# Layer 0's feed-forward with its modulation and gate moved to ScalarE, between transposes

## The chip, the core and the metric

The kernel runs on one core of a Trainium2 chip. The metric is device time in microseconds for one execution of the whole program. The engines are named by their units: TensorE (PE in the profile, PEld for its weight loads), VectorE (DVE), ScalarE (ACT), GpSimd (POOL) and SyncE (SP, here only for transfers).

## The reference, cut to what matters

Two transformer layers with adaptive layer norm, on x of 8 batches x 512 tokens x 128 features, in float32. Each layer adds a gated attention and then a gated feed-forward. The change is in layer 0's feed-forward, whose linear layers quantise inputs and weights to four-bit floats in blocks of 16 features:

```python
def fp4_quant_dequant(x):
    xb = x.reshape(shape[:-1] + (shape[-1] // 16, 16))
    scale = jnp.max(jnp.abs(xb), axis=-1, keepdims=True) / 6.0
    scale = jnp.maximum(scale, jnp.float32(1e-12))
    xn = xb / scale
    idx = jnp.searchsorted(_MID, jnp.abs(xn))
    q = _GRID[idx] * jnp.sign(xn) * scale      # grid 0, 0.5, 1, 1.5, 2, 3, 4, 6
    return q.reshape(shape)

def fp4_linear(x, w):
    return jnp.einsum('bsk,nk->bsn', fp4_quant_dequant(x), fp4_quant_dequant(w))

# layer 0, feed-forward: 128 -> 352 -> 128
h = _layernorm(x, axis=-1) * (1 + cb) + sb     # sb, cb, gb: 128 values per batch
gate, y = fp4_linear(h, w_gate), fp4_linear(h, w_up)
x = x + gb * fp4_linear(jax.nn.silu(gate) * y, w_down)
```

The six vectors per batch (sa, ca, ga for attention, sb, cb, gb for the feed-forward) come from one small product with a conditioning input.

## The kernel before

The residual stream X lies in SBUF for the whole run, tokens in rows (partitions): for each of the 8 batches, NT = 4 tiles of 128 tokens x 128 features. The run has four stages one after the other: layer 0's attention (to 156 us), layer 0's feed-forward (158 to 307 us), layer 1's attention (to some 920 us), and layer 1's feed-forward.

In layer 0's attention a scheduler orders the instructions of each engine by data and by its own costs. In layer 0's feed-forward the order is the one written out in the program (`tc.manual_schedule()`), so an engine that waits for one instruction holds all that stand behind it in its queue.

The modulation vectors exist in two forms. `modT[0]` has features in partitions, one column per kind and batch. `modb[0]` has them laid out as rows, the same in every partition: `mod_rows` makes them per batch, with a diagonal tile on GpSimd (L353), a matmul with ones (L358) and a copy by ScalarE (L362), for four kinds: attention's gate, the feed-forward's shift, scale and gate.

The feed-forward of a batch goes through these parts, each of class `Ffn0`:

- `norm`: ScalarE normalises the four tiles into `n` (L295); GpSimd multiplies by the scale row (L589) and adds the shift row (L590).
- `Fp4.scales` on VectorE: maxima per block of 16 (L426), scale (L430), its reciprocal (L433, L436). The input of one batch and the hidden `y` of an earlier one share these instructions.
- `Fp4.scaled`: the input times its reciprocal scales, on GpSimd (L439). `octaves`: an Abs on ScalarE (L446). `rounded`: two passes on VectorE (L450, L451). `back`: times the scales (L454), on VectorE for the input, on GpSimd for `y` in most batches.
- `turn`: four transposes (L311) into PSUM and a copy by ScalarE (L596) to `hT`, features in partitions.
- `products(t)` for each of four token tiles: gate and up matmuls (L609, L610), SiLU on ScalarE (L612), their product on VectorE (L613) into `y`, 352 features per token.
- `y` is quantised as the input was.
- `down(t)`: four transposes of 88 x 128 (L627) and a copy by ScalarE (L628) to `yT`.
- `gated`: GpSimd multiplies the down weights by the batch's gate row (L634). `last(t)`: the down projection (L640) into PSUM tile `pd`, tokens in rows. `end`: VectorE adds it to X (L647).

The batches are pipelined. In step i the loop works on batch i-1 (`past`: down projection), i (`cur`: rounding of `y`), i+1 (`new`: products), i+2 (`far`: quantising and turning the input) and i+3 (`next_far`: norm). The inputs of the first AHEAD = 3 batches are already quantised during layer 0's attention, where they are called `hq`; the others are called `n_f`. Between these parts, some steps place work of layer 1's first batch (`more_front`): norms, projections and products of line coordinates, the latter on GpSimd (L756). After each batch's `end`, VectorE takes layer 1's statistics of it (L231, L232), in front of the next step's `scales`. After the loop, a hand-written tail treats batches 6 and 7.

PSUM has four buffers of tag "mm" (products), two of "tp" (transposes) and two of "acc" (`pd`).

Of the kernel before, what the change touches and what calls it, by code (L numbers as in the profile page):

```python
# [11 lines left out]
F32 = mybir.dt.float32  # L12
# [3 lines left out]
AF = mybir.ActivationFunctionType  # L16
ALU = mybir.AluOpType
AX = mybir.AxisListType
PSUM = bass.MemoryType.PSUM

P = 128
# [17 lines left out]
def kernel(ctx: ExitStack, tc: tile.TileContext, a: dict, out: bass.AP):  # L39
# [15 lines left out]
    def acc(name):  # L55
        return four.tile([P, 512], F32, tag="acc", bufs=accs, name=name)
# [160 lines left out]
    class Stats:  # L217


        def __init__(self, tag):  # L220
            self.tag, self.mv, self.rstd, self.nb = tag, [], [], []
# [85 lines left out]
    def transposed(src, name, pt=None):  # L307

        pt = tp(name) if pt is None else pt
        for t in range(NT):  # L310
            nc.tensor.transpose(pt[:, t * P : (t + 1) * P], src[:, t, :], ident)  # L311
        return pt
# [34 lines left out]
    def mod_rows(l, b):  # L347

        mb = modb[l][:, b]
        nch = mb.shape[1]  # L350
        cols = modT[l][:, 2:6, b] if l == 0 else modT[l][:, 2::3, b]
        diag = sp.tile([P, nch, P], F32, tag=f"diag{l}", bufs=1, name=f"diag{l}_{b}")
        nc.gpsimd.tensor_mul(  # L353
            diag, ident.unsqueeze(1).to_broadcast([P, nch, P]),
            cols.unsqueeze(2).to_broadcast([P, nch, P]),
        )
        pb = mm(f"modb{l}_{b}")
        nc.tensor.matmul(  # L358
            pb[:, : nch * D], lhsT=ones, rhs=diag.rearrange("p j d -> p (j d)"),
            start=True, stop=True,  # L360
        )
        nc.scalar.copy(mb.rearrange("p j d -> p (j d)"), pb[:, : nch * D])  # L362

    modulation(0, wmod0, 4)
    nc.sync.dma_start(out=wmod1, in_=a["wmod1"])


# [14 lines left out]
    def rows(ap, n):  # L382

        return ap.unsqueeze(1).to_broadcast([ap.shape[0], n, D])
# [12 lines left out]
    class Fp4:  # L397

        def __init__(self, pool, src, np_, n, name):
            self.pool, self.np_, self.n, self.name, self.x = pool, np_, n, name, src
            self.blocks = src.rearrange("p (g k) -> p g k", k=16)

        def over(self, v):
            return v.unsqueeze(2).to_broadcast([self.np_, self.n // 16, 16])
# [6 lines left out]
        def scales(self, *more):  # L413

            all_ = (self, *more)
            num = [q.n // 16 for q in all_]
            nb, np_ = sum(num), self.np_
            amax, scale, rs = (
                self.pool.tile(
                    [P, nb], F32, tag=f"q_{tag}_b{nb}", bufs=bufs, name=f"q_{tag}_{self.name}"  # L420
                )[:np_]
                for tag, bufs in (("amax", 1), ("scale", 2), ("rs", 2))
            )
            parts = [slice(sum(num[:i]), sum(num[: i + 1])) for i in range(len(num))]
            for q, part in zip(all_, parts):
                nc.vector.tensor_reduce(  # L426
                    amax[:, part], q.blocks, AX.X, ALU.max, apply_absolute_value=True
                )
                q.scale, q.rs = scale[:, part], rs[:, part]
            nc.vector.scalar_tensor_tensor(  # L430
                scale, amax, 1.0 / 6.0, tiny[:np_].to_broadcast([np_, nb]), ALU.mult, ALU.max
            )
            nc.vector.reciprocal(rs, scale)  # L433


            nc.vector.scalar_tensor_tensor(rs, rs, 2.0 ** -24 - 1.0, rs, ALU.mult, ALU.min)  # L436

        def scaled(self, eng=nc.gpsimd):
            eng.tensor_mul(self.blocks, self.blocks, self.over(self.rs))  # L439

        def octaves(self):

# [136 lines left out]
    class Ffn0:  # L579
# [5 lines left out]
        def norm(self, n=None):  # L585

            b = self.b
            self.n = n = ln_norm(self.pool, "f0", self.stats, b, n)
            nc.gpsimd.tensor_mul(n, n, rows(modb[0][:, b, 2, :], NT))  # L589
            nc.gpsimd.tensor_add(n, n, rows(modb[0][:, b, 1, :], NT))  # L590
            self.qh = Fp4(self.pool, n.rearrange("p t d -> p (t d)"), P, NT * D, f"h_{b}")

        def turn(self):
            pt = transposed(self.qh.x.rearrange("p (t d) -> p t d", d=D), f"q0T_{self.b}")
# [34 lines left out]
                self.yT[:, :, t * P : (t + 1) * P], pt[:CH0].rearrange("p (c q) -> p c q", q=P)  # L629
            )  # L630

        def gated(self):
            self.wd = self.pool.tile([CH0, NC0, D], F32, tag="wd", name=f"wd_{self.b}")
            nc.gpsimd.tensor_mul(self.wd, w0[2], rows(modb[0][:CH0, self.b, 3, :], NC0))  # L634

        def last(self, t):
            if t == 0:
                self.po = acc(f"pd_{self.b}")
            for c in range(NC0):
                nc.tensor.matmul(  # L640
                    self.po[:, t * P : (t + 1) * P], lhsT=self.yT[:, c, t * P : (t + 1) * P],
                    rhs=self.wd[:, c, :], start=(c == 0), stop=(c == NC0 - 1),
                )

        def end(self):
            xb = X[:, self.b * NT : (self.b + 1) * NT, :]
            nc.vector.tensor_add(xb, xb, self.po.rearrange("p (t d) -> p t d", d=D))  # L647

    flag = const.tile([1, 1], I32, name="flag")
    nstats, w0, f0 = Stats("f0"), [], []  # L650
# [157 lines left out]
    with tc.tile_pool(name="p_f0", bufs=2) as pool, tc.manual_schedule():  # L808
        for f in f0:
            f.pool = pool  # L810
        f0 += [Ffn0(pool, b, stats) for b in range(AHEAD, B)]


        front, lines = fronts1(keep, st, 0, nstats, packs)
        steps = {
            2: ((front,), (front,)),
            3: ((front,), (front,)),
            4: ((lines,), (front,)),
            5: ((lines,), (front,)),
            6: ((lines,), (lines, lines, front)),  # L820
        }

        def f0_at(i):
            return f0[i] if 0 <= i < B else None

        for i in range(-2, B - 1):
            past, cur, new, far, next_far = (f0_at(i + k) for k in range(-1, 4))

            def more_front(half):
                for series in steps.get(i, ((), ()))[half]:
                    next(series)

            open_ = far if far and far.b >= AHEAD else None
            if next_far and next_far.b < AHEAD:
                next_far = None
            quants = (cur.qy if cur else []) + ([open_.qh] if open_ else [])
            if quants:
                quants[0].scales(*quants[1:])  # L840
            if open_:
                open_.qh.scaled()
            if cur:
                cur.qy[0].scaled()
                cur.gated()
            if new:
                new.products(0)
                new.products(1)
            if next_far:
                next_far.norm()  # L850
            if past:
                past.down(0)
                past.down(1)
            if open_:
                open_.qh.octaves()
                open_.qh.rounded()
                open_.qh.back(nc.vector)
            more_front(0)
            if new:
                new.products(2)  # L860
            if past:
                past.last(0)
                past.down(2)
            if new:
                new.products(3)
            if past:
                past.last(1)
                past.down(3)
            if i == B - 2:
                new.qy[0].scales()  # L870
                new.qy[0].scaled(nc.vector)
            if cur:
                cur.qy[0].octaves()
                cur.qy[0].rounded()
                cur.qy[0].back(nc.vector if i > B // 2 else nc.gpsimd)
            if past:
                past.last(2)
            if far:
                far.turn()
            if past:  # L880
                past.last(3)
                past.end()
            more_front(1)
            if past:
                nstats.after(past.b)


        past, cur = f0[B - 2 :]
        qa, qb = cur.qy
        cur.gated()  # L890
        act_tables()
        qa.octaves()
        past.down(0)
        past.down(1)
        qb.scales()
        qb.scaled()
        qa.rounded()
        qa.back(nc.vector)
        next(lines)
        past.last(0)  # L900
        past.down(2)
        past.last(1)
        past.down(3)
        qb.octaves()
        qk_packs(packs, 1)
        past.last(2)
        past.last(3)
        past.end()
        next(lines)
        next(lines)  # L910
        cur.down(0)
        cur.down(1)
        qb.rounded()
        qb.back(nc.vector)
        cur.last(0)
        cur.last(1)
        next(front)
        cur.down(2)
        nstats.after(past.b)
        cur.last(2)  # L920
        cur.down(3)
        cur.last(3)
        cur.end()
        nstats.after(cur.b)
    stats = nstats
# [740 lines left out]
```

## Time and profile before

| | |
|---|---|
| runs | 1119.83, 1113.53 and 1120.34 us; median 1119.83 |
| profiled execution | 1115.72 us, of which 1114.0 us are the span of the profile |
| busy, share of the span | PE 87%, DVE 73%, PEld 66%, ACT 51%, POOL 45% |
| mean granted TensorE clock | 0.954 |
| layer 0's feed-forward | 158 to 307 us |

The span reaches from the first to the last instruction. Busy shares are means over all four stages, which differ in what limits them. Lines of instructions give the start, the time, engine, source line, operation, output and inputs with their shapes, and in brackets how long the engine stood idle before and what released it. The granted clock is TensorE's; 0.50 is half of full speed.

### The profile page before, as it was taken

What the parts mean: (1) busy time and instruction counts of PE and PEld (TensorE: products, weight loads), DVE (VectorE), ACT (ScalarE), POOL (GpSimd) and SP (SyncE); (2) the same over time, 40 slices, a digit from 0 to 9 for tenths busy, and PEclk for the clock granted to TensorE, in tenths of its full rate; (3) what the DMA queues carried; (4) which work ended last, traced back from release to release, by engine and by line L of the source; (5) the groups of instructions that cost most, each with busy time, mean ns of one, the idle gap of its engine ahead of it and who ended that gap; (6) DMA issues with size and microseconds to landing.
All of it is one profiled execution on the core that took longest, in us unless ns stands there. A gap on an engine that the chain in (4) does not pass through costs nothing.

```text
span 1114.0 us, 24810 instructions
## 1 busy us (share of the span) xinstructions
PE 966.2 (87%) x10474; PEld 730.2 (66%) x10474; DVE 812.1 (73%) x1548; ACT 571.8 (51%) x863; POOL 502.1 (45%) x577
## 2 busy tenths in 40 slices
PE   5788886867678999999999989999988887999996
PEld 3566654655545677767777677677766675787885
DVE  7887968999847778787787877877877836645633
ACT  4736444644422545555545455454545447867743
POOL 4436217774456666576665665656644400000000
PEclk9899999898757999999999999999999999999998
DMA  6011000000000000000000000000000000000001
GB/s 174 29 39 29 1 1 1 1 1 1 1 0 1 2 3 2 2 2 3 2 2 2 3 2 2 2 2 2 2 2 2 2 2 1 1 1 20 19 1 40
DMA packets 14713, 11.19 MB, mean 10 GB/s; under 512 B 2246, under 2 KB 13062, under 8 KB 14598
## 3 DMA queue, kind: packets, MB, share of 16 engines
q1 hardware_dynamic: 13878, 8.96, 2.8%
q8 instruction: 84, 1.38, 0.5%
q10 hardware_dynamic: 720, 0.60, 0.2%
q14 instruction: 31, 0.25, 0.1%
HBM read 7.46 MB, written 2.10 MB: 9 GB/s over the span
## 4 chain that ended last, share of the span: by engine, by line
PE 52%; DVE 15%; ACT 14%; POOL 11%; issue 6%; DMA 1%; SPq 0%; POOLq 0%; ACTq 0%; DVEq 0%
PE ph L1134 11%; ACT pr L1071 7%; PE s L1056 6%; PE s L1016 6%; PE s L1044 5%; PE pi L989 3%; POOL kd L970 3%; PE po L1085 3%; POOL bias L1005 2%; PE py L494 2%; PE s L501 1%; POOL m L756 1%; DVE pack_q L1033 1%; PE po L1534 1%; PE pmT L944 1%
## 5 line engine op out<-in xcount | busy, mean ns | idle before, releaser
L1071 ACT ACTIVATE pr<-s 128x1024 f32<-128x1024 f32 (+1 forms) x192 | 169.0, 880 | 237.4 <-PE s L1056 237.4
L1033 DVE TENSOR_REDUCE pack_q<-s 128x2 f32<-128x256 f32 (+3 forms) x256 | 205.4, 824 | 6.6
L1056 PE MATMUL s<-qm,kd 32*128 32x128 f32 x2560 | 195.0, 286 | 0.0
L1016 PE MATMUL s<-kd,qd 31*128 31x256 f32 (+3 forms) x1024 | 187.3, 475 | 2.4 <-POOL bias L1005 1.5
L1030 DVE TENSOR_TENSOR s<-s,bias 128x256 f32<-128x256 f32 (+1 forms) x192 | 99.4, 517 | 84.9 <-PE s L1056 63.9
L1056 PEld LDWEIGHTS s<-qm,kd 32*128 32x128 f32 x2560 | 158.4, 187 | 1.3 <-issue 1.3
L1044 PE MATMUL s<-ident,bias 128*128 128x128 f32 x512 | 96.2, 290 | 46.3 <-ACT pr L1071 42.5
L1005 POOL TENSOR_SCALAR_AFFINE_SELECT bias<-bias 128x512 f32<-128x512 f32 x128 | 77.8, 634 | 102.0 <-DVE bias L1001 101.7
L970 POOL TENSOR_TENSOR kd<-k1T,dk 128x512 f32<-128x512 f32 (+3 forms) x128 | 106.7, 866 | 37.7 <-ACT k1T L961 37.7
L1044 PEld LDWEIGHTS s<-ident,bias 128*128 128x128 f32 x512 | 55.4, 141 | 92.3 <-ACT pr L1071 79.1
L1134 PE MATMUL ph<-g,h 128*128 128x512 f32 x448 | 106.7, 396 | 0.0
L1016 PEld LDWEIGHTS s<-kd,qd 31*128 31x128 f32 x1024 | 83.9, 189 | 33.5 <-issue 20.1
L1001 DVE TENSOR_TENSOR bias<-pi,wdiag 128x512 f32<-128x512 f32 x128 | 79.5, 683 | 34.6 <-PE pi L989 34.6
L1134 PEld LDWEIGHTS ph<-g,h 128*128 128x128 f32 x448 | 83.7, 188 | 19.9
L1085 PE MATMUL po<-pr,pack_v 128*32 128x128 f32 x2560 | 89.8, 276 | 3.9 <-DVE o L1105 3.7
L951 POOL TENSOR_TENSOR qd<-q1T,dq 128x512 f32<-128x512 f32 x32 | 40.6, 1269 | 88.4 <-ACT q1T L939 88.4
L1085 PEld LDWEIGHTS po<-pr,pack_v 128*32 128x32 f32 x2560 | 64.4, 109 | 17.6 <-PE s L1056 5.8
L989 PE MATMUL pi<-k1L,q1T 31*128 31x128 f32 x1024 | 54.7, 288 | 0.9 <-DVE pack_q L1033 0.9
L989 PEld LDWEIGHTS pi<-k1L,q1T 31*128 31x128 f32 x1024 | 47.8, 195 | 8.0 <-issue 7.2
L1524 DVE TENSOR_TENSOR g<-g2v,g 128x1024 fp32r<-128x1024 f32 x16 | 19.6, 1226 | 38.2 <-ACT g L1520 38.2
L951 POOL TENSOR_TENSOR qm<-m1T,dq 128x512 f32<-128x512 f32 x32 | 40.6, 1270 | 13.7 <-ACT m1T L978 13.7
L439 POOL TENSOR_TENSOR y<-y,q_rs_y 128x1408 f32<-128x1408 f32 (+1 forms) x8 | 20.1, 2510 | 46.0 <-DVE q_rs_y L436 23.5
(332 smaller groups left out, 1973.1 us busy)
## 6 DMA issues: line engine op xcount, KB each, us to landing
X<-in_x SPq DMA_DIRECT2D x8, 256.0 KB, 4.1
w<-in_h SPq DMA_DIRECT2D x8, 256.0 KB, 2.6
out_x<-X SPq DMA_DIRECT2D x8, 256.0 KB, 2.3
w<-in_w SPq DMA_DIRECT2D x3, 256.0 KB, 4.5
wmod<-in_wmod ACTq DMA_DIRECT2D x1, 384.0 KB
wmod<-in_wmod SPq DMA_DIRECT2D x1, 384.0 KB, 5.3
c_wqkv<-in_wqkv ACTq DMA_DIRECT2D x1, 192.0 KB, 5.6
c_wA<-in_wA SPq DMA_DIRECT2D x1, 192.0 KB, 4.5
```

The source lines that it names most:

```text
L951: nc.gpsimd.tensor_mul(qd, qT.rearrange("p (t q) -> p t q", q=P), dq[:, g, :].unsqueeze(1).to_broadcast([P, NT, P]),)
L970: nc.gpsimd.tensor_mul(kd[t], kT[:, : (t + 1) * P], dk[:, g, 384 - t * P :])
L989: nc.tensor.matmul(pi[:, j, tile_t], lhsT=qT[rl, tile_t], rhs=kL[rl, tile_t], start=True, stop=True,)
L1005: nc.gpsimd.affine_select(out=bias[:, j], in_=bias[:, j], compare_op=ALU.is_ge, fill=NEG, base=0, pattern=[[0, NT], [-1, P]], channel_mult ...
L1016: nc.tensor.matmul(s[:, j, at : at + (t + 1) * P], lhsT=st["qd", b, g][rk, t, :], rhs=st["kd", b, g][t][rk, :], start=True, stop=True,)
L1030: nc.vector.tensor_add(diag, diag, tiles)
L1033: nc.vector.tensor_reduce(packs["q", b % 2][:, t, h : h + 2, KM], s[:, :, at : at + (t + 1) * P], AX.X, ALU.max, negate=True,)
L1044: nc.tensor.matmul(p[:, j, at + t * P : at + (t + 1) * P], lhsT=bias[:, j, t, :], rhs=ident, is_transpose=True, start=(n == 0), stop=False ...
L1056: nc.tensor.matmul(p[:, j, at + k * P : at + (k + 1) * P], lhsT=st["kd", b, g][t][rk, k * P : (k + 1) * P], rhs=st["qm", b, g][rk, t, :], ...
L1071: nc.scalar.activation(pr[:, :, :end], st["p", b, g, u, i][:, :, :end], AF.Exp)
L1085: nc.tensor.matmul(po[32 * j : 32 * j + 32, t * P : (t + 1) * P], lhsT=vp[:, k, h * VW : h * VW + 32], rhs=st["pr", b, g, u, j // 2][:, j ...
L1134: nc.tensor.matmul(dst[:, j], lhsT=w, rhs=src[part][:, j], start=first and part == 1, stop=last and part == 0,)
```

## The change

Shift, scale and gate of layer 0's feed-forward are applied by ScalarE with features in partitions, where they are one scale and one bias per partition, instead of by GpSimd with rows.

- For batches 3 to 7, `norm` ends after ScalarE's normalising. A new part `modulated` transposes the normalised tiles (TensorE, four transposes), and ScalarE applies scale and shift while it moves them out of PSUM into a tile `m`. A new part `turned_back` transposes `m` back, into a PSUM tile of tag "acc". The quantiser takes its maxima from this PSUM tile and its scaling reads it and writes to SBUF; this scaling is now on VectorE (`scaled(nc.vector)`).
- The down projection swaps its operands, so that `pd` has features in partitions; it uses the plain down weights. `gated` is now a ScalarE activation that multiplies `pd` by the gate into a tile `o`; `end` transposes `o` (four transposes) and VectorE adds that PSUM tile to X.
- The gate is no longer laid out as a row: `mod_rows` makes three kinds for layer 0.
- The order in the loop: `y`'s scaling comes first on GpSimd; the third `products` and the first `more_front` come ahead of the input's rounding; `modulated` ahead of the rounding of `y`; the last two `last` and `gated` ahead of `turn`; `turned_back` behind it. In the tail, batch 6's `end` comes behind the first `down` of batch 7.

```diff
-        cols = modT[l][:, 2:6, b] if l == 0 else modT[l][:, 2::3, b]
+        cols = modT[l][:, 2:5, b] if l == 0 else modT[l][:, 2::3, b]
...
-    modulation(0, wmod0, 4)
+    modulation(0, wmod0, 3)
...
-        def __init__(self, pool, src, np_, n, name):
-            self.pool, self.np_, self.n, self.name, self.x = pool, np_, n, name, src
-            self.blocks = src.rearrange("p (g k) -> p g k", k=16)
+        def __init__(self, pool, src, np_, n, name, dst=None):
+
+            self.pool, self.np_, self.n, self.name = pool, np_, n, name
+            self.x = src if dst is None else dst
+            self.src, self.blocks = (
+                ap.rearrange("p (g k) -> p g k", k=16) for ap in (src, self.x)
+            )
...
-                    amax[:, part], q.blocks, AX.X, ALU.max, apply_absolute_value=True
+                    amax[:, part], q.src, AX.X, ALU.max, apply_absolute_value=True
...
         def scaled(self, eng=nc.gpsimd):
-            eng.tensor_mul(self.blocks, self.blocks, self.over(self.rs))
+            eng.tensor_mul(self.blocks, self.src, self.over(self.rs))
...
             self.n = n = ln_norm(self.pool, "f0", self.stats, b, n)
+            if b >= AHEAD:
+                return
             nc.gpsimd.tensor_mul(n, n, rows(modb[0][:, b, 2, :], NT))
...
+        def modulated(self):
+
+            pt = transposed(self.n, f"nT_{self.b}")
+            self.m = self.pool.tile([P, NT, P], F32, tag="m", bufs=1, name=f"m_{self.b}")
+            nc.scalar.activation(
+                self.m.rearrange("p t q -> p (t q)"), pt, AF.Identity,
+                bias=modT[0][:, 3, self.b : self.b + 1], scale=modT[0][:, 4, self.b : self.b + 1],
+            )
+
+        def turned_back(self):
+            name = f"mT_{self.b}"
+            pt = transposed(self.m, name, acc(name))
+            self.qh = Fp4(
+                self.pool, pt, P, NT * D, f"h_{self.b}", self.n.rearrange("p t d -> p (t d)")
+            )
...
-        def gated(self):
-            self.wd = self.pool.tile([CH0, NC0, D], F32, tag="wd", name=f"wd_{self.b}")
-            nc.gpsimd.tensor_mul(self.wd, w0[2], rows(modb[0][:CH0, self.b, 3, :], NC0))
-
...
-                    self.po[:, t * P : (t + 1) * P], lhsT=self.yT[:, c, t * P : (t + 1) * P],
-                    rhs=self.wd[:, c, :], start=(c == 0), stop=(c == NC0 - 1),
-                )
+                    self.po[:, t * P : (t + 1) * P], lhsT=w0[2][:, c, :],
+                    rhs=self.yT[:, c, t * P : (t + 1) * P], start=(c == 0), stop=(c == NC0 - 1),
+                )
+
+        def gated(self):
+            self.o = self.pool.tile([P, NT, P], F32, tag="o", bufs=1, name=f"of_{self.b}")
+            nc.scalar.activation(
+                self.o.rearrange("p t q -> p (t q)"), self.po, AF.Copy,
+                scale=modT[0][:, 5, self.b : self.b + 1],
+            )
 
         def end(self):
             xb = X[:, self.b * NT : (self.b + 1) * NT, :]
-            nc.vector.tensor_add(xb, xb, self.po.rearrange("p (t d) -> p t d", d=D))
+            pt = transposed(self.o, f"oT_{self.b}")
+            nc.vector.tensor_add(xb, xb, pt.rearrange("p (t d) -> p t d", d=D))
...
-            if open_:
-                open_.qh.scaled()
             if cur:
                 cur.qy[0].scaled()
-                cur.gated()
+            if open_:
+                open_.qh.scaled(nc.vector)
...
+            more_front(0)
+            if new:
+                new.products(2)
             if open_:
                 open_.qh.octaves()
                 open_.qh.rounded()
                 open_.qh.back(nc.vector)
-            more_front(0)
-            if new:
-                new.products(2)
...
+            if next_far:
+                next_far.modulated()
...
             if past:
                 past.last(2)
+                past.last(3)
+                past.gated()
             if far:
                 far.turn()
+            if next_far:
+                next_far.turned_back()
             if past:
-                past.last(3)
                 past.end()
...
         past.last(3)
-        past.end()
+        past.gated()
         next(lines)
         next(lines)
         cur.down(0)
+        past.end()
         cur.down(1)
...
         cur.last(3)
+        cur.gated()
         cur.end()
```

More of the change, by code (lines that the diff above doesn't have):

```diff
@@ L889 @@
         qa, qb = cur.qy
-        cur.gated()
         act_tables()
```

## The prediction

> **What bounds the kernel now.** I read the page first (busy shares, the 40 slices), then the chain of work that ended last, then stretches of some 18 us with their busy times, then the timeline of one stretch engine by engine, and the answers by source line. The page says that TensorE leads over the whole run, which hides that the stage the change touches, layer 0's feed-forward, has another limit:
>
> ```profile
> span 1114.0 us, 24810 instructions
> ...
> PEclk9899999898757999999999999999999999999998
> ```
>
> The feed-forward runs from 158 to 307 us. Its busy times by stretch (columns: length, then busy us and count of PE, PEld, DVE, ACT, POOL, then the granted clock) show VectorE full and TensorE not:
>
> ```profile
> 194.00:212.00 18.00, 14.68 (x69) 11.61 (x70) 16.39 (x23) 11.73 (x23) 13.61 (x10) 0.73 0.00 0
> 212.00:230.00 18.00, 14.97 (x89) 11.59 (x87) 16.61 (x25) 10.53 (x21) 12.71 (x7) 0.98 0.00 1
> 250.00:272.00 22.00, 15.22 (x80) 11.93 (x81) 20.47 (x30) 10.69 (x21) 8.98 (x7) 0.84 0.00 0
> ```
>
> The chain agrees: in this stage it runs almost wholly through VectorE. Here is VectorE in the step whose reciprocal scales are ready at 216.36 us, and GpSimd beside it:
>
> ```profile
> 216.08 0.28 DVE L436 SCALAR_TENSOR_TENSOR q_rs_y<-q_rs_y 128x120 f32<-128x120 f32 x1
> 216.28 0.94 DVE L613 TENSOR_TENSOR y<-silu,pu 128x352 f32<-128x352 f32 x2
> 218.20 2.40 DVE L450 SCALAR_TENSOR_TENSOR n_f<-q_big_h,n_f 128x512 f32<-128x512 bf16 x1 [0.97 <-ACT q_big_h L446]
> 220.64 1.64 DVE L451 SCALAR_TENSOR_TENSOR n_f<-q_big_h,n_f 128x512 f32<-128x512 bf16 x1
> 222.31 1.65 DVE L454 TENSOR_TENSOR n_f<-n_f,q_scale_y 128x512 f32<-128x512 f32 x1
> 223.88 0.94 DVE L613 TENSOR_TENSOR y<-silu,pu 128x352 f32<-128x352 f32 x2
> 224.75 1.83 DVE L450 SCALAR_TENSOR_TENSOR y<-q_big_y,y 128x1408 f32<-128x1408 bf16 x1
> 226.61 1.62 DVE L451 SCALAR_TENSOR_TENSOR y<-q_big_y,y 128x1408 f32<-128x1408 bf16 x1
> ```
>
> ```profile
> 217.46 2.59 POOL L439 TENSOR_TENSOR y<-y,q_rs_y 128x1408 f32<-128x1408 f32 x1
> 220.01 1.71 POOL L634 TENSOR_TENSOR wd<-wdT,mb 88x512 f32<-88x512 f32 x1
> 221.69 1.72 POOL L589 TENSOR_TENSOR n_f<-n_f,mb 128x512 f32<-128x512 f32 x1
> 223.49 1.60 POOL L590 TENSOR_TENSOR n_f<-n_f,mb 128x512 f32<-128x512 f32 x1
> ```
>
> Three passes over 512 columns take 2.40, 1.64 and 1.65 us; they end at 220.60, 222.28 and 223.96, each 0.55 after one of GpSimd's ends (220.05, 221.72, 223.41). The same L450 elsewhere, and L613, which reads one operand from PSUM, by source line (min/median/max ns):
>
> ```profile
> L450 DVE SCALAR_TENSOR_TENSOR hq<-q_big_h,hq x3: 680/693/1323, 105.9 to 128.3; 128x512 f32<-128x512 bf16 x3
> ...
> L613 DVE TENSOR_TENSOR y<-silu,pu x32: 506/512/523, 160.0 to 276.8; 128x352 f32<-128x352 f32 x32
> ```
>
> So VectorE with two SBUF operands waits its turn with GpSimd (0.69 us of work became 2.40); with a PSUM operand it does not (506 to 523 ns whatever GpSimd does).
>
> What lies next below that limit is the row of ScalarE behind TensorE. The Abs of y (L446) sits behind the last copy of yT, that behind the transposes, and these behind the up-projection of the fourth tile, which waits for VectorE's first product (PSUM slot):
>
> ```profile
> 222.31 0.58 ACT L628 COPY yT<-yTp 88x512 f32<-88x512 f32 x1 [1.46 <-PE yTp L627]
> 222.79 1.38 ACT L446 ACTIVATE q_big_y<-y 128x1408 bf16<-128x1408 f32 x1
> ```
>
> ```profile
> 234.72 0.86 PE L609 MATMUL pg<-wgT,hqT 128*128 128x352 f32 x2 [0.17 <-DVE y L613]
> ```
>
> The stage's end is TensorE's and goes on into layer 1's first transposes:
>
> ```profile
> 304.40 1.76 PE pd L640 x8
> 306.16 0.02 issue
> 306.19 0.70 DVE X L647
> 306.89 0.04 issue
> 306.93 1.13 PE n1T L311 x4
> ```
>
> **The change part by part.**
>
> *GpSimd loses work.* Per full step wd (1.71), the two modulations (1.72, 1.60) and the scaling of n_f (1.06): 6.1 us. It is off the path itself; its worth is that L450, L451, L454 on n_f meet only the scaling of y (2.59). After that they cost 0.69, 0.66, 0.68 (hq rows) rather than 5.7.
>
> *VectorE gains one pass*, the scaling of n_f out of PSUM. No such row; nearest is the add out of PSUM, L647, 0.68 us (0.61 start to start); bounds 0.5 (L613) and 1.1 (GpSimd's own). I take 0.61. The maximum out of PSUM: attention's maxima from PSUM took 0.69, the SBUF one 0.68, so nothing.
>
> *TensorE gains* three times four transposes per batch (0.44 us for four at full clock, 1.07 at half). The down projection keeps its number of matmuls (only operands swap).
>
> *ScalarE gains* m and o: 0.78 us for a 128x512 activation with scale and bias out of PSUM (L706), 0.75 taken for o. m stands ahead of the Abs of y. o waits for the last down projection; behind it on ScalarE is the copy of hqT, which the next products wait for, and behind the transposes of o on TensorE are those products. They have some 2 us to spare, since the transposes of y wait for GpSimd's 2.59.
>
> *A full step walked through,* from scales ready (0): n_f scaled to 0.61; two products to 1.55, the third to 2.1; GpSimd's scaling of y runs 0.1 to 2.73, so L450 on n_f ends near 3.3, L451 3.97, L454 4.65, fourth product 5.1. Meanwhile TensorE: fourth tile's gate and up from 1.2 (first product plus hop) to 2.35, down projection to 3.25, transposes to 3.7; ScalarE: copy of yT to 4.35, m to 5.1, Abs of y to 6.5. VectorE stands idle 1.4, then 1.57 and 1.64 on y (9.75), residual 0.6, statistics 1.7, next scales 3.7: 15.8 us, against 17.9 before. Without that idle time it would be 14.3, and 13.7 with no turn taken with GpSimd either.
>
> *All steps.* Ends of y's rounding before, and by the same walk after:
> first (round y of batch 0, scales at 179.6): 178.4, since L450 and L451 (2.49, 2.57) lose GpSimd's load (−1.8) and the Abs comes 0.85 later behind m;
> 191.55 → 190.6 (no gain in the step: TensorE at half clock and m ahead of Abs);
> 210.37 → 208.0 (two table loads and layer 1's norms ahead of the third SiLU hold ScalarE; gbias and the add to X now meet n_f);
> 228.23 → 223.95;
> 246.91 → 240.45 (layer 1's line products on GpSimd, 2.6 unhindered, now meet n_f and cost back 1.5);
> 269.11 → 259.95 (no m here; before, L451 on n_f took 3.48 behind the same kind of products);
> 287.45 → 276.7 (no wd: L430 2.33 and L436 0.73, held by it, shrink).
> Gain so far 10.75.
>
> *The tail loses.* For batch 6, o (0.75) and its transposes come between; VectorE's residual add stands ahead of the rounding of batch 7's second half and goes from 297.0 to some 298.3, the rounding with it; the transposes behind it wait until 301.85 rather than 300.87: +1.0. For batch 7 o and four transposes stand bare before the last add: 0.75 + 0.45 to 1.07 + hops 0.1 = +1.7 taken. Total +2.7.
>
> *Attention of layer 0.* Three modulation rows rather than four: of the 0.88 us of matmul a quarter (0.22) and 0.11 of the 0.58 copy; the chain shows this pair ahead of hT in about six batches: −2.0. The scheduler also reorders transposes, norms and the quantisation of the first three batches here; nearest measure is the 2.5 us that VectorE stood before a maximum of hq, so bounds −3 and +3 on this; I take 0.
>
> *Sum.* −10.75 + 2.7 − 2.0 = −10.0. The profiled execution took 1115.72 (span 1114.0 and 1.7 around it): 1105.7. It lies 4.1 below the median 1119.83 of runs from 1113.53 to 1120.34; the same sum from the median gives 1109.8. I predict 1107.5.
>
> **Rivals.**
> *A, the forecast:* 1101 to 1113, as the uncertain terms go (attention ±3, tail ±1, hops and half-clock spells ±2).
> *B, less comes back:* ScalarE's row (m, Abs, o, copy) is tighter than walked, each step near 17. For: ScalarE is served in order and every row there waits for TensorE. Against: it is busy 10.5 of 18 us. Five steps lose 1.2 more: 1113.5.
> *C, VectorE alone sets the step:* Abs ready in time, 14.3 a step, which is 1.45 less in four steps (5.8), and 2 more from attention: 1100. For: transposes may run closer than their rows. Against: the walk puts the Abs 1.4 late.
> *D, slower: TensorE falls to half clock through the stage.* Its part of the loop, from the first transposes of y to the last, is 5.9 us at full clock, 11.8 at half; about 0.95 is hidden, so +5 in each of five steps, and +2 at the end: 1132. It outweighs the gain once the loop's TensorE work grows by 3 us a step, a clock of about 0.67. For: the stage's clock is 0.73 in one stretch, and the tail runs cold. Against: half clock followed idle times of 4.7 and 4.9 us; after 1.9 it held 0.98, and the longest idle time walked here is 2.2.
> [...]
> That the change does nothing: the order of instructions shows GpSimd's four instructions gone, so no.
>
> **Chances.** A 0.52, B 0.20, C 0.16, D 0.12. About 1% is what a measurement of this kernel can tell, so faster means below 1108.6: three fifths of A (0.32) and C: 0.48. The rest of A, B and a little of D: 0.42. Slower by 1%: 0.10. The range, 1098 to 1121, holds nearly all of A and B and two thirds of C, some 0.8; D and the far end of C are left out.
>
> **What would show it.** Right: L450 on n_f near 1.2 us with its wait, L451 and L454 near 0.68; steps of 15.5 to 16.5; VectorE idle before L450 on y, released by the Abs; last add of batch 7 near 298. Wrong: these three still above 1.5; half clock in more than one stretch; a bare wait on o in every step.

## The result, and the profile after

The changed kernel took 1104.49 us (median of 4 runs, 1102.38 to 1106.04) beside 1118.71 for the kernel before (4 runs): a ratio of 0.9872, 95% interval 0.9847 to 0.9897. Run once more with more rounds it took 1109.64 (6 runs, 1104.43 to 1110.44) beside 1119.58: 0.9893, 0.9865 to 0.9922. So it is 1.1 to 1.3% faster, 12 to 14 us by these ratios. The first profiled execution after took 1103.96, the one before 1115.72.

The page of the profile after, its span and the granted clock:

```profile
span 1102.2 us, 24959 instructions
...
PEclk9899999998658999999999999999999999999998
```

The stretch from 212 to 230, as shown of before (columns as there: length, then busy us and count of PE, PEld, DVE, ACT, POOL, then the clock); the step lies 5.7 us earlier in it now:

```profile
212.00:230.00 18.00, 15.81 (x103) 12.75 (x103) 15.36 (x27) 11.13 (x22) 6.81 (x4) 1.00 0.01 1
```

What counts here is POOL, 6.81 us rather than 12.71, DVE 15.36 rather than 16.61, PE 0.84 and ACT 0.60 more. VectorE in the step whose scales are ready at 210.67, with GpSimd and ScalarE beside it:

```profile
210.71 0.69 DVE L443 TENSOR_TENSOR n_f<-mT,q_rs_y 128x512 f32<-128x512 f32 x1
...
212.94 1.02 DVE L454 SCALAR_TENSOR_TENSOR n_f<-q_big_h,n_f 128x512 f32<-128x512 bf16 x1
213.99 0.69 DVE L455 SCALAR_TENSOR_TENSOR n_f<-q_big_h,n_f 128x512 f32<-128x512 bf16 x1
214.72 0.69 DVE L458 TENSOR_TENSOR n_f<-n_f,q_scale_y 128x512 f32<-128x512 f32 x1
...
217.75 1.62 DVE L454 SCALAR_TENSOR_TENSOR y<-q_big_y,y 128x1408 f32<-128x1408 bf16 x1 [1.91 <-ACT q_big_y L450]
219.41 1.63 DVE L455 SCALAR_TENSOR_TENSOR y<-q_big_y,y 128x1408 f32<-128x1408 bf16 x1
```

```profile
210.82 2.59 POOL L443 TENSOR_TENSOR y<-y,q_rs_y 128x1408 f32<-128x1408 f32 x1 [3.48 <-PE pg L631]
```

```profile
215.68 0.78 ACT L603 ACTIVATE m<-nT,mt 128x512 f32<-128x512 f32 x1
216.35 1.37 ACT L450 ACTIVATE q_big_y<-y 128x1408 bf16<-128x1408 f32 x1
```

The three passes on n_f took 2.40, 1.64 and 1.65 before; they take 1.02, 0.69 and 0.69. The first still meets the scaling of y, which ends at 213.41; the other two meet nothing. The scaling of n_f out of PSUM (L443, 0.69) runs beside GpSimd's 2.59 and is not held. (The releaser that the POOL line names is not what it waited for; the scales were ready at 210.67.) Then VectorE stands for 1.91 us until the Abs of y is there, which follows m on ScalarE.

All kernels below are read by four stretches of their profile: when VectorE makes its first feed-forward product (attention before it), from there to the end of the last full rounding of y (batch 6, with the multiplication by its scales), from there to the start of the last add to X (the tail), and from there to the end of the span.

| profile | first product | to last full rounding | tail | rest | span |
|---|---|---|---|---|---|
| before | 160.01 | 127.43 | 18.75 | 807.8 | 1114.0 |
| after | 157.18 | 115.17 | 23.06 | 806.8 | 1102.2 |
| after, again | 157.39 | 116.94 | 21.76 | 812.5 | 1108.6 |
| load put back | 157.26 | 125.69 | 21.90 | 806.3 | 1111.1 |
| before, load left out | 161.73 | 118.06 | 18.11 | 812.1 | 1110.0 |
| gate part alone | 157.67 | 120.88 | 21.83 | 811.6 | 1112.0 |
| modulation part alone | 162.81 | 120.54 | 18.42 | 805.5 | 1107.3 |
| Abs moved | 157.91 | 108.66 | 21.31 | 815.0 | 1102.9 |
| before, Abs moved | 158.76 | 127.63 | 18.17 | 806.8 | 1111.4 |
| one row | 155.23 | 116.97 | 21.76 | 812.3 | 1106.3 |
| gate in rows, late | 158.45 | 113.85 | 25.14 | 805.6 | 1103.0 |
| gate in rows, early | 157.60 | 120.77 | 18.99 | 806.2 | 1103.6 |
| TensorE filled | 156.27 | 118.97 | 20.72 | 810.7 | 1106.7 |
| joined | 155.98 | 113.65 | 18.17 | 806.4 | 1094.2 |

The rest has code that the edits leave alone (but for one product at its start in the filled kernel), and still it is 805.5 to 807.8 in eight profiles and 810.7 to 815.0 in six, the changed kernel on both sides. So it can differ between executions of one program, which is told at the end; the verdicts on mechanisms below rest on the first three columns. There is one profile of each kernel but the changed one, whose two differ by 1.8 us in the second column and by 1.3 in the third.

### The profile page after: what moved, and what is told of

The parts are those of the page before. It is cut to its first block, busy times and chain, and to the rows that moved or that the text cites. A ratio compares the mean times of both kernels' runs of the same rounds, so it can differ in the third digit from the quotient of the medians.

```text
span 1102.2 us, 24959 instructions
## 1 busy us (share of the span) xinstructions
PE 970.0 (88%) x10546; PEld 735.5 (67%) x10546; DVE 796.9 (72%) x1553; ACT 578.2 (52%) x876; POOL 464.8 (42%) x554
## 4 chain that ended last, share of the span: by engine, by line
PE 55%; ACT 15%; DVE 12%; POOL 11%; issue 6%; DMA 1%; SPq 0%; POOLq 0%; ACTq 0%; DVEq 0%
PE ph L1165 11%; ACT pr L1102 7%; PE s L1087 6%; PE s L1047 6%; PE s L1075 5%; PE pi L1020 3%; POOL kd L1001 3%; PE po L1116 3%; POOL bias L1036 2%; PE py L498 2%; PE pd L658 2%; PE s L505 1%; POOL m L782 1%; DVE pack_q L1064 1%; PE po L1565 1%
## 5 line engine op out<-in xcount | busy, mean ns | idle before, releaser
L443 POOL TENSOR_TENSOR y<-y,q_rs_y 128x1408 f32<-128x1408 f32 (+1 forms) x8 | 20.0, 2503 | 62.8 <-DVE q_rs_y L440 36.7
```

## The experiments

### Is it GpSimd's load?

*Load put back* (changed kernel):

```
+spare = pool.tile([P, NT, D], F32, tag="spare", bufs=1, name="spare")
+nc.gpsimd.memset(spare, 1.0)
...
 cur.qy[0].scaled()
+nc.gpsimd.tensor_mul(spare[:CH0], spare[:CH0], rows(modb[0][:CH0, 0, 2, :], NT))
+if open_ and next_far:
+    nc.gpsimd.tensor_mul(spare, spare, rows(modb[0][:, 0, 2, :], NT))
+    nc.gpsimd.tensor_add(spare, spare, rows(modb[0][:, 0, 1, :], NT))
```

> The changed kernel, with GpSimd's three instructions per step (88x512 product, 128x512 product, 128x512 sum) put back on a scratch tile right behind the scaling of y; nothing reads the tile, and the modulation and the gate stay on ScalarE. Theory 1, VectorE's passes over two SBUF operands wait their turn with GpSimd: the three passes on n_f go from 0.69 each back to 1.6 to 2.4, y's rounding is held too where GpSimd is still busy, each of five steps grows by 1 to 2.5, and most of the gain is gone: 1110 to 1116. Theory 2, the gain comes from attention and from the new order of the instructions, GpSimd being off the path: the passes stay at 0.69 or the step hides them, 1104 to 1106.

Measured: 1111.33, ratio 0.9947 (0.9921 to 0.9974). VectorE in the step whose scales are ready at 213.46, and GpSimd:

```profile
217.44 0.69 DVE L454 SCALAR_TENSOR_TENSOR n_f<-q_big_h,n_f 128x512 f32<-128x512 bf16 x1
218.16 1.64 DVE L455 SCALAR_TENSOR_TENSOR n_f<-q_big_h,n_f 128x512 f32<-128x512 bf16 x1
219.84 1.65 DVE L458 TENSOR_TENSOR n_f<-n_f,q_scale_y 128x512 f32<-128x512 f32 x1
```

```profile
216.16 1.27 POOL L871 TENSOR_TENSOR spare<-spare,mb 88x512 f32<-88x512 f32 x1
217.50 1.75 POOL L873 TENSOR_TENSOR spare<-spare,mb 128x512 f32<-128x512 f32 x1
219.33 1.60 POOL L874 TENSOR_TENSOR spare<-spare,mb 128x512 f32<-128x512 f32 x1
```

L455 ends at 219.80 and L458 at 221.49, 0.55 and 0.56 after one of GpSimd's ends (219.25, 220.93), although they share no data. It is the pattern of before, made again by a tile that nothing reads. (L454 meets nothing in this step: it stands behind a product that came late, after 1.95 us of waiting for TensorE.) From the first product to the last full rounding the time went from 115.17 (116.94 in the second profile) to 125.69: 8.8 to 10.5 of the 10.5 to 12.3 us that the change had gained there. Summed over this stretch, the three passes on n_f take 22.6 us rather than 15.0 and the two roundings of y 25.1 rather than 22.7, together 9.9 more, while VectorE's idle time is 15.3 beside 14.5 and 16.3 in the two profiles of the changed kernel. So the loss lies in the held passes and not in waits. Theory 1 holds. The kernel keeps the new order of the instructions and ScalarE's part; the 1.7 by which it is still shorter than before is what these two can be worth together in the steps.

*Before, load left out* (`norm` returns ahead of the two modulations from batch 3 on; `gated` reuses batch 0's `wd`):

> The kernel before, in its own order, with GpSimd's three instructions left out from batch 3 on: the scale and shift of those batches are left out, and the gated down-projection weight of batch 0 serves all batches. Nothing is put in their place, so neither ScalarE nor TensorE gets work. Theory 1 (turns with GpSimd): the three passes on n_f fall to 0.7 to 1.2, the last full rounding of y ends 9 to 12 earlier than 287.45, attention and the tail stay: 1106 to 1110. Steps shorter than those of the changed kernel by about 1 would say that ScalarE's row costs that there. Theory 2 (the order and attention): within 2 of before, 1117 to 1120.

Measured: 1107.72, ratio 0.9911 (0.9878 to 0.9944), inside theory 1's span. The steps lose 9.4 us (118.06). The last full rounding ends 7.7 earlier rather than 9 to 12, since the first product came 1.7 later (161.73), and one of the three passes did not fall. The steps are not shorter than those of the changed kernel, which do more work (115.17 and 116.94). This line says why, in the step whose scales are ready at 215.02:

```profile
216.91 2.40 DVE L450 SCALAR_TENSOR_TENSOR n_f<-q_big_h,n_f 128x512 f32<-128x512 bf16 x1 [1.03 <-ACT q_big_h L446]
```

With n_f scaled on GpSimd ahead of y, the Abs of n_f comes 1.03 us late, and the first pass still meets the scaling of y. In the changed kernel VectorE scales n_f itself and y's scaling starts at once: that row is 0.68 to 1.02 there, with no wait. So moving the scaling seems worth the 0.61 it costs VectorE, and about what ScalarE's new work costs besides. Part of this is the new order: with the gate part alone, where n_f is scaled on GpSimd too but a third product stands ahead of the first pass, the wait is 0.29 and the pass again 2.40. No run separates the two.

### Which half of the change?

*Gate part alone* (no `modulated` and `turned_back`; n_f's scaling on GpSimd, first) and *modulation part alone* (`wd` and four rows as before):

> The gate part alone: gate by ScalarE between transposes, three modulation rows, the third product ahead of n_f's rounding; modulation and n_f's scaling by GpSimd in rows as before. Theory 1: GpSimd keeps 4.4 of 6.1 us per step, so one of the three passes on n_f is freed: first product about 2.5 earlier (attention), steps shorter by 0.5 to 1.5, tail longer by 4.3 as in the changed kernel: 1112 to 1117. Theory 2 (attention and order are the gain): nearly the whole gain is here, 1104 to 1108.

> The modulation part alone: modulation by ScalarE between transposes, the input quantised out of PSUM; the gate stays in the weight (GpSimd's 88x512 product behind the scaling of y) with four modulation rows. Theory 1: GpSimd loses 4.4 of 6.1 us per step, steps near those of the changed kernel but for one pass that meets the 1.7 us product; no gain in attention (first product near 160.0) and no loss in the tail (18.7 from the last full rounding of y to the last add): 1106 to 1111. Theory 2: 1115 to 1120, since attention's part is missing.

Measured: gate 1110.04, 0.9934 (0.9910 to 0.9957); modulation 1109.17, 0.9918 (0.9892 to 0.9944). In the steps the gate gives 6.55 and the modulation 6.89, together 13.4, where both at once give 12.26 and 10.49: nearly additive, as far as one profile of each can say (each of the two also has its part of the new order). The gate gives 1.3 a step, near the top of what was written, and its total came below the span of 1112 to 1117. The tail went the way expected: 21.83 with the gate on ScalarE, 3.1 longer than before where 4.3 was written, and 18.42 without. The first product came at 157.67 with three rows; with four it came at 162.81, where about 160.0 was expected. Theory 2 would have put nearly all of the gain into one of them, and falls.

### What limits it now?

*Abs moved* (changed kernel), and the same in the *before* kernel:

```
 new.products(3)
+if cur:
+    cur.qy[0].octaves()
 if past:
     past.last(1)
     past.down(3)
...
 if cur:
-    cur.qy[0].octaves()
     cur.qy[0].rounded()
```

> The changed kernel with one instruction moved: ScalarE's Abs of y stands right behind the fourth SiLU of the step, ahead of the last two copies of yT and of m. Theory 1, after the change ScalarE's row behind TensorE sets the step where n_f's passes are unhindered: VectorE's idle time before y's rounding (3.30 in the first full step, 1.91 in the third) goes to 0.5 or less, and the part of it that the residual add does not give back by waiting for oT is gained: 2 to 4.5 less, last full rounding of y near 268.5, 1100 to 1103. Theory 2, the idle time only moves to the residual add or to the maximum: 0 to 1 less.

> The kernel before with that one instruction moved: the Abs of y behind the fourth SiLU. Theory 1, before the change VectorE's passes on n_f, held by GpSimd, cover ScalarE's row, so its place costs nothing there: steps within 0.3 each, VectorE without idle time ahead of y's rounding, 1115 to 1119. Theory 2, the place of the Abs is worth as much here as in the changed kernel: 4 to 7 less.

Measured: in the changed kernel 1097.32, ratio to before 0.9785 (0.9736 to 0.9833); in the kernel before 1116.14, 0.9983 (0.9960 to 1.0005). ScalarE and VectorE of the changed kernel with the Abs moved, in the step whose scales are ready at 206.89:

```profile
210.22 1.37 ACT L450 ACTIVATE q_big_y<-y 128x1408 bf16<-128x1408 f32 x1
...
212.27 0.78 ACT L603 ACTIVATE m<-nT,mt 128x512 f32<-128x512 f32 x1
```

```profile
211.97 1.62 DVE L454 SCALAR_TENSOR_TENSOR y<-q_big_y,y 128x1408 f32<-128x1408 bf16 x1
...
215.45 0.69 DVE L673 TENSOR_TENSOR X<-X,oT 128x512 f32<-128x512 f32 x1 [0.19 <-PE oT L311]
```

The Abs now starts where ScalarE stood waiting for the next yT, y's rounding has no wait, and of the 1.91 only 0.19 comes back, at the add. The steps take 108.66 rather than 115.17 or 116.94: more than I had written, since the first rounding of y also loses 0.87 of waiting (1.92 became 1.05), and the step with 3.30 of idle time is 3.7 shorter. In the kernel before the same move changes nothing (127.63 against 127.43; there VectorE is busy with the held passes when the Abs ends). So it gains only where GpSimd's load is gone.

### The tail

*Gate in rows, late* and *early* (changed kernel; `wd` of the last two batches as before, by GpSimd behind the second half's scaling, or behind the scaling of y in the step before and, for batch 7, at the start of the tail):

> The changed kernel with the gate of the last two batches in the weight again, as before (GpSimd's 88x512 product, four modulation rows for those two batches). Theory 1, the tail's loss is o, its transposes and the TensorE work that they make late: from the last full rounding of y to the last add 23.06 goes back to 18.5 to 19.5, attention pays up to 0.7 for two rows: 1100 to 1102. Theory 2, the tail is long because it runs at half clock, whatever stands in it: 21.5 to 22.5, since only o (0.69) and oT go: 1102 to 1104.

> The changed kernel with the gate of the last two batches in the weight again, the GpSimd products now early: right behind the scaling of y in the step before, and ahead of the tail. Theory 1, o, oT and what they make late are the tail's loss: from the last full rounding of y to the last add 18.2 to 19.5 rather than 23.06, 2 to 4 less in all unless a half-clock spell falls elsewhere. Theory 2, the tail is long because of the clock it is granted: above 21.

Measured: late 1109.06 (0.9891, 0.9842 to 0.9941), early 1105.30 (0.9869, 0.9838 to 0.9900). The late one missed: in its tail TensorE waited 6.05 us for wd, which stood behind GpSimd's scaling, so it says nothing on the question. The early one answers it: the tail is 18.99, as long as before, so o, oT and what they make late are the loss. But the step in which GpSimd makes wd grew from 16.66 to 18.40: 0.8 of it in two small VectorE instructions that GpSimd holds (L434 1.18 to 1.44, L440 0.20 to 0.74; they end at 271.36 and 272.60, 0.06 and 0.08 after one of GpSimd's ends), 0.96 in a longer wait for the last up-projection. So 0.8 at least of the 2.8 to 4.1 is given back, and the total does not separate this kernel from the changed one.

*TensorE filled* (changed kernel; `warm` is n products of ident and wgT that nothing reads):

```
+warm(7)
 past.down(0)
...
+warm(1)
 cur.down(2)
+warm(1)
 nstats.after(past.b)
 cur.last(2)
 cur.down(3)
+warm(1)
 cur.last(3)
 cur.gated()
+warm(2)
 cur.end()
+warm(1)
```

> The changed kernel with 13 products of 128x352 that nothing reads put into TensorE's row in the tail, where it waits (seven in the 4.5 us ahead of the last full rounding's transposes, then one or two at each wait). Theory 1, the half clock of the tail and of the stage behind it (0.50 from 290 to 337) comes from idle time between short pieces of TensorE work: with the gaps filled the clock stays near 1.0 up to the last add, pd falls from 2.08 to about 1.1 and oT from 1.11 to about 0.6, the tail is 2 to 3 shorter, and layer 1 starts at the full clock for some microseconds more: 1098 to 1102. Theory 2, idle time is not what sets it, or the added work stands in the way: within 1 of the changed kernel or up to 2 slower.

Measured: 1111.52, 0.9915 (0.9877 to 0.9953): in all not faster than the changed kernel. TensorE at the end of the tail, changed kernel first, filled second:

```profile
291.35 2.08 PE L658 MATMUL pd<-yT,wdT 88*128 88x128 f32 x8 [0.67 <-ACT yT L650]
294.26 1.11 PE L311 MATMUL oT<-ident,of 128*128 128x128 f32 x4 [0.84 <-ACT of L665]
```

```profile
293.14 1.16 PE L658 MATMUL pd<-yT,wdT 88*128 88x128 f32 x8
...
295.32 0.60 PE L311 MATMUL oT<-ident,of 128*128 128x128 f32 x4
```

Locally theory 1 holds in part. The clock between 272 and 290 is 1.00 rather than 0.78 or 0.72 in the two profiles of the changed kernel, and the tail is 20.72 rather than 21.76 or 23.06. The gain on pd (1.16 rather than 2.08) and oT (0.60 rather than 1.11) is one over the first profile alone: in the second, with nothing filled, they took 1.16 and 0.66, and the first transposes at half clock there are those of n1T at 296.84 (1.12). The total does not show the gain: the steps ahead of the added work happened to be 2 to 4 us longer in this execution (118.97, with 3.30 of idle time ahead of y's rounding in two steps), and its rest was one of the long ones. Whether filling pays in the median stays open.

### Attention, and the joined version

*One row* (changed kernel; `nch = 1 if l == 0 and b >= AHEAD else modb[l].shape[2]`):

> The changed kernel with one modulation row rather than three for batches 3 to 7 in layer 0's attention (the scale and shift rows of these batches are read by nothing any more). Theory 1, each row costs its share of matmul, copy and diagonal on attention's path: the fourth row was worth 2.8 over eight batches, so ten more rows are worth 3 to 4: first product near 153.5, 1100 to 1102. Theory 2, the row was not on the path, and the first product moved by the order that the scheduler chose: 155 to 159, 1102 to 1107.

Measured: 1107.55, 0.9869 (0.9817 to 0.9920). The first product came at 155.23, 2.0 earlier, half of what I expected and inside theory 2's span as well; the total does not separate it from the changed kernel. Inconclusive.

*After, again* and *joined* (Abs moved, one or two rows from batch 3 on, gate of the last two batches in rows, early):

> The changed kernel once more, beside the next three. If half-clock spells fall differently in each execution, its profile keeps the same VectorE passes on n_f, while VectorE's idle times ahead of y's rounding move between about 0 and 3.3 and the stretch from layer 1's attention to the last stage is either near 690 or near 696 after the last add: 1102 to 1112. If the spells belong to the kernel's order, all of these stay within 0.3 of the first profile: 1102 to 1106.

> Joined: Abs of y behind the fourth SiLU, one modulation row for batches 3 to 5 and two for the last two, and the gate of the last two batches in the weight with early GpSimd products. If the three effects add up: steps as with the Abs moved (108.7 from the first product to the last full rounding, rather than 115.2), tail 18.2 to 19.5 rather than 23.06, attention 1 to 2 less: 1090 to 1094. If the tail and attention give nothing: 1095 to 1098.

Measured: joined 1093.80 (6 runs, 1090.16 to 1103.94), 0.9773 (0.9732 to 0.9813). Tail (18.17) and attention (155.98) came as expected; the steps are 113.65, not 108.7: 1.7 went to the step with wd, the rest to steps in which the add waited up to 1.28 for oT or the Abs came 0.58 late. The interval overlaps that of the Abs moved alone. Both are faster than the kernel before by a little over 2%, where the intervals do not exclude 2%, and than the changed kernel by about 1%. The changed kernel's second profile has the long rest (812.5) and two other idle times, as the first expectation there said.

## Why the prediction was right, step by step

The time was forecast at 1107.5 (1098 to 1121); it measured 1104.5 and 1109.6. By terms, against before, first profile and second:

- *Steps*: forecast −10.75; measured −12.26 and −10.49. The mechanism, VectorE's turns with GpSimd, is shown by the load put back. In the first profile the passes on n_f gave 14.6 us and the roundings of y 3.5; the scaling out of PSUM took 3.5 back, and 3.2 went into more idle time. Inside the step two things came out otherwise. The first pass on n_f was 0.68 to 1.02; the second and third were 0.69 in two steps of five but 1.46 to 1.65 and 0.83 to 1.22 in three, where gbias, the add to X or layer 1's line products run on GpSimd. And the idle time ahead of y's rounding, walked as 1.4 in the full step, was 3.30, 0.16, 1.91 and then nothing in the last two full steps, where those held passes cover it. That the sum came out this close is in part luck, because these miss in opposite ways; the second profile, with idle times of 2.27, 0.19 and 3.30, gives another sum.
- *n_f out of PSUM*: taken 0.61, measured 0.69 long and 0.61 from start to start. *o*: taken 0.75, measured 0.67 to 0.69.
- *Tail*: forecast +2.7; measured +4.3 and +3.0. The second one and four others with the same tail (load put back, gate alone, Abs moved, one row) lie at 21.3 to 21.9, which is +2.6 to +3.2. The excess in the first profile is the clock of 0.50 from 290 on, which fell into it there; in the second the stretch from 290 to 310 had 0.65.
- *Attention*: forecast −2.0; measured −2.8 and −2.6. Over all profiles the first product is at 158.8 to 162.8 with four rows (four profiles, mean 160.8) and 156.3 to 157.9 with three (six, mean 157.3): −3.5. The term was mis-sized, by its durations: it had 0.33 a batch, from the matmul (0.22) and the copy (0.11). By the means before and after, the two records of the matmul went from 770 to 621 ns each (0.30), the copy from 584 to 479 (0.11), and the diagonal on GpSimd, which the term left out, from 1063 to 854 (0.21): 0.62, or 3.7 over six batches. That all of it lay on the path was not shown.
- *Rest*: forecast nothing; −1.0 and +4.7, by the execution and not by the code (last section).

*Rival B* (ScalarE's row tighter) was right for two steps of each profile, with idle times of 1.91 to 3.30, which is where the Abs moved finds its gain. *Rival C* named the step that VectorE alone allows, 14.3; with the Abs moved, the step from 200.90 to 215.25 took 14.35, the two beside it 16.86 and 16.00. In the changed kernel that step took 16.36, and the Abs moved shows that the order on ScalarE was the reason.

*Rival D* (half clock through the stage) did not come: in the five stretches from 176 to 272 (bounds 194, 212, 230 and 250) the mean granted clock was 0.88 to 1.00 in the first profile and 0.87 to 1.00 in the second, beside 0.73 to 0.98 before. But half clock did come inside the steps, in spells of 3 to 7 us: before the change, for example, from 206 to 212 (0.50) and from 260 to 267 (0.53), after it from 174 to 177 (0.50), 191 to 194 (0.50) and 242 to 245 (0.52) in the first profile. In the second the step from 203.63 to 223.13 (ends of y's rounding) took 19.50 us, where it took 16.36 in the first: VectorE stood 1.46 and 0.77 us in it for up-projections, and 3.30 rather than 1.91 ahead of y's rounding; the stretch from 194 to 212 had 0.87 there rather than 0.99, the one from 212 to 230 0.94 rather than 1.00. The prediction argued against D that half clock followed idle times of 4.7 and 4.9 us and not one of 1.9. The traces show no such bound: the spell before the change at 206 came with an idle time of TensorE of 2.36 us, while one of 2.60 ahead of 250.84 in the same profile was followed by the full clock (1.00 from 250 to 253). In the first profile of the changed kernel TensorE stood for 2.37 ahead of 190.64, with half clock from 191 on, and for 1.92 ahead of 207.40, with 1.00 from 207 to 212. No run here tells what the added transposes alone do to the clock, since the filling was of ordinary products.

## What to carry to other kernels

Where a pass of VectorE over two SBUF operands takes more than twice its usual time (here 1.64 rather than 0.69 us), look for ends of GpSimd's instructions just ahead of its own end (here by 0.55). Here it paid to take that work to other engines, even at the price of more instructions there. After such a change read which row the freed engine waits for, and put the instruction it waits for at the first idle place of its engine; here that one line was worth 6.5 to 8.3 us in the steps, beside the change's 10.5 to 12.3, and nothing before it. A change that puts work in front of the last link of a stage is to be costed there by itself, since a step elsewhere can hide what a tail cannot.

## What the runs showed that I had not expected

The same program has a rest of 806.8 us in one execution and 812.5 in another. The clock of one stretch of it, first and second profile of the changed kernel:

```profile
870.00:890.00 20.00, 17.14 (x296) 13.43 (x299) 15.45 (x29) 10.57 (x16) 3.69 (x5) 1.00 0.01 2
```

```profile
870.00:890.00 20.00, 17.17 (x236) 13.25 (x237) 14.79 (x32) 9.44 (x14) 3.69 (x5) 0.83 0.01 2
```

TensorE is busy for as long in both and gets 1.00 in one and 0.83 in the other, with 296 and 236 matmuls on record. The runs of the kernel before vary by as much: of the 19 beside the first four experiments 12 took 1114.1 to 1117.5 and 7 took 1119.4 to 1122.8. None lay between there, but the 17 beside the last experiments, 1113.3 to 1122.9, show no such gap, so a split into two groups is not shown. Two profiles of these kernels may thus differ by 6 us with no cause in the code, and a part's worth is safer read from its own stretch than from the total. What makes the clock fall in one execution and not in another no run here shows. The idle times close ahead do not tell it: in the first profile it fell to 0.50 at 290 after gaps of at most 0.88 us, with TensorE busy 3.45 of the 5 us before; in the second the same instructions, with gaps of 0.86 and 0.67 us, still took 1.16 (pd, at 293.40) and 0.66 (oT, at 295.40), as at the full clock, beside 2.08 and 1.11 in the first.
